# Patch layer of a four-layer network on one Trainium2 core: the product with C is cut in two, the rest is done after the next scan, and two decay buffers become one ring tile

## The chip, the cores and the metric

The kernel runs on one core of a Trainium2 chip. The metric is device time in microseconds (us), from the start to the end of the launch. Five engines work side by side, each in the order of its own queue: PE (matmul), DVE (VectorE: elementwise work and scans), ACT (ScalarE: activations and copies), POOL (GpSimd: elementwise work in SBUF) and SP (here it only issues DMAs). An instruction of one engine that needs another engine's result waits for a semaphore to reach a count.

## The reference, cut to what matters

Four layers are applied to x of shape (8, 96, 64, 64). Only layer 2 (the third), the "patch layer", is touched. It projects x to 192 inner channels, samples them at shifted positions, cuts the image into 256 small patches of 4 by 4 positions and runs a selective scan over the 16 positions of each patch, in four directions k, for 192 channels d and 16 states n:

```
delta = softplus(dts + bias)                        # (patch, k, d, l)
A = -exp(A_logs)                                    # (k, d, n)
def step(hst, inputs):
    ut, dt, bt, ct = inputs
    dA  = exp(dt[..., None] * A)                    # the decay
    hst = hst * dA + (dt * ut)[..., None] * bt      # the scan
    y   = einsum('bkdn,bkn->bkd', hst, ct)          # product with C, summed over the states
    return hst, y
```

Then come a sum over the four directions, a layer norm, a gate and an output projection with a residual.

## The kernel before

All work in fp32. Layer 2 handles 8 images in 8 chunks of 512 positions (32 patches), 64 chunks in all. A chunk has 48 **groups**: 4 directions x 2 halves of the channels x 6 blocks of 16 channels. One group has 128 partitions (16 channels x 8 states) and 1024 columns: two halves of 512, one for states 0 to 7 and one for 8 to 15. Its steps are:

- **dd**: SP starts a 512 KB DMA that spreads delta and delta*u over the 128 partitions (L320), four slots ahead, into one of 5 buffers.
- **decay**: two ACT activations, exp(delta*A), 128x512 each, into a PSUM tile `da` of two banks (L328).
- **dbu**: POOL multiplies delta*u with B (L349), two slots ahead, 6 buffers.
- **scan**: DVE runs one scan over the 1024 columns, in place in `da` (L1453). Directions 2 and 3 run backwards.
- **product**: DVE multiplies the scan's result with C, into `dbu` (L358).
- **total**: PE sums over the states with two matmuls (L366), one slot later.

For three groups of a chunk, called `late`, the scan writes to an SBUF tile `h`, POOL does the product (L354), and the total comes one slot later still.

The order is written out by hand. `Slots.slot(t)` issues slot t: the dd of group t+4, the two decays of group t+1, the side work "join" and "first", the scan of t, the total of t-1, the side work "pe", the total of a late t-2, the side work "act", the dbu of t+2, the late product of t-1, the side work "pool", the product of t, and the side work "dve", "sp", "end". All other steps of the layer (norm, offset convolution, sampling, softplus, gates, output) are side work, put into slots by `sl.at(slot, kind, run)`. Nothing reorders the instructions of an engine; a framework adds the waits between them. It keeps account of who wrote and read each tile.

`da` comes from a pool `psd` with two buffers, so each group's `da` is a tile of its own:

```
g.da = new(self.psd, [128, 2, NW], "ps_d")
```

Layer 0 uses the same class `Slots` for its own scans.

Of the kernel before, what the change touches and what calls it, by code (L numbers as in the profile page):

```python
# [12 lines left out]
AF = mybir.ActivationFunctionType  # L13
ALU = mybir.AluOpType
PSUM = bass.MemoryType.PSUM
# [3 lines left out]
CH = 96  # L19
IH = IW = 64  # L20
NP = IH * IW
NW = 512
NC = NP // NW
DI = 192
HD = 96
NG = 6
# [12 lines left out]
class Names:  # L39


    def __init__(self):
        self.n = 0
# [6 lines left out]
new = Names()  # L50
# [187 lines left out]
LOG_EXP = "natural_log_exp_and_others"  # L238
FAR = 1e25
AHEAD = 4  # L240


def log_exp_tables(S):
# [31 lines left out]
class Slots(Plan):  # L275
# [12 lines left out]

    def __init__(self, S, consts, pool, psd):
        super().__init__(S)
        self.pool, self.psd = pool, psd
        self.red = S.load("k_red", consts)
        self.consts = consts
        self.minus = new(consts, [128, 1], "minus")
        S.nc.vector.memset(self.minus, -1.0)
        self.half = new(consts, [128, 1], "half")
        S.nc.vector.memset(self.half, 0.5)
        self.groups = {}  # L300
# [6 lines left out]
        return a  # L307

    def run(self):
        ts = list(self.plan) + [t + d for t in self.groups for d in (-AHEAD, 1)]  # L310
        with self.S.tc.manual_schedule():
            for t in range(min(ts), max(ts) + 1):
                self.slot(t)

    def slot(self, t):
        nc, G = self.S.nc, self.groups.get
        g = G(t + AHEAD)
        if g:
            g.dd = new(self.pool, [128, 2, NW], "dd", bufs=AHEAD + 1)
            nc.sync.dma_start(  # L320
                g.dd.rearrange("p x l -> p (x l)"),
                g.steps().unsqueeze(1).to_broadcast([GC, HS, 2 * NW]),
            )
        g = G(t + 1)
        if g:
            g.da = new(self.psd, [128, 2, NW], "ps_d")
            for i in range(2):
                nc.scalar.activation(  # L328
                    g.da[:, i, :], g.dd[:, 0, :], AF.Exp, scale=g.a[:, i : i + 1]
                )  # L330
        for what in ("join", "first"):
            self.side(t, what)
        g = G(t)
        if g:
            g.h = new(self.pool, [128, 2, NW], "h", bufs=2) if g.late else g.da
            flat = [v.rearrange("p s l -> p (s l)") for v in (g.h, g.da, g.dbu)]
            g.scan(*flat)
        g = G(t - 1)
        if g and not g.late:
            self.total(g)  # L340
        self.side(t, "pe")
        g = G(t - 2)
        if g and g.late:
            self.total(g)
        self.side(t, "act")
        g = G(t + 2)
        if g:
            g.dbu = new(self.pool, [128, 2, NW], "dbu", bufs=6)
            nc.gpsimd.tensor_tensor(  # L349
                g.dbu, g.dd[:, 1:2, :].to_broadcast([128, 2, NW]), g.b(), ALU.mult  # L350
            )
        g = G(t - 1)
        if g and g.late:
            nc.gpsimd.tensor_tensor(g.dbu, g.h, g.c(), ALU.mult)  # L354
        self.side(t, "pool")
        g = G(t)
        if g and not g.late:
            nc.vector.tensor_tensor(g.dbu, g.h, g.c(), ALU.mult)  # L358
        for engine in ("dve", "sp", "end"):
            self.side(t, engine)  # L360

    def total(self, g):

# [642 lines left out]
def layer2(S, src, dst, st_in, st_out, images):  # L1006
    tc, nc = S.tc, S.nc
    with ExitStack() as ctx:
        cp = ctx.enter_context(tc.tile_pool(name="l2c", bufs=1))
        psd = ctx.enter_context(tc.tile_pool(name="l2q", bufs=2, space=PSUM))  # L1010
        psy = ctx.enter_context(tc.tile_pool(name="l2y", bufs=1, space=PSUM))
        psk = ctx.enter_context(tc.tile_pool(name="l2k", bufs=1, space=PSUM))
        psa = ctx.enter_context(tc.tile_pool(name="l2p", bufs=1, space=PSUM))
# [37 lines left out]
        with tc.tile_pool(name="l2t", bufs=1) as tp:  # L1051
# [10 lines left out]
            for n in range(4):  # L1062
                at = slice(432 * n, 432 * n + 432)
# [35 lines left out]

        fp = ctx.enter_context(tc.tile_pool(name="l2f", bufs=1))  # L1100
        wp = ctx.enter_context(tc.tile_pool(name="l2w", bufs=1))
        sl = Slots(S, cp, wp, psd)
        log_exp_tables(S)
        acol = sl.negative_exp("l2_alog")

# [22 lines left out]
        def turned(v):  # L1128

            return v.rearrange("p (n h w) -> p n w h", h=4, w=4)  # L1130

        def front(ch, b, pad, xs, c, B):
# [22 lines left out]
                nc.gpsimd.memset(pad[:, r, :], 0.0)  # L1155

            sl.at(B - 92, "sp", load)
            sl.at(B - 89, "act", normal)
            if c in (0, NC - 1):
                sl.at(B - 89, "pool", border)  # L1160

            def conv(m, k0, k1):
                def run():
# [24 lines left out]

            for m, slots, last in (
                (0, ((-86, 2), (-85, 2), (-84, 2), (-81, 2), (-80, 1)), -79),  # L1190
                (1, ((-79, 2), (-67, 2), (-66, 1), (-62, 2), (-61, 2)), -60),
            ):
                k = 0
                for t, taps in slots:
                    sl.at(B + t, "pe", conv(m, k, k + taps))
                    k += taps
                sl.at(B + last, "first", conv_out(m))
# [80 lines left out]
            for t, run in (  # L1278
# [2 lines left out]
                (-47, down), (-46, sampled),  # L1281
            ):
                sl.at(B + t, "pool", run)
            sl.at(B - 44, "act", lambda: nc.scalar.copy(xs[:CH, 1, :], turned(xs[:CH, 0, :])))

            def inner(j):


                def pe():
                    ch["pa"] = new(psa, [128, NW], "ps_a")  # L1290
                    nc.tensor.matmul(
                        ch["pa"],
                        wuu.rearrange("c m o -> c (m o)")[:, j * 128 : (j + 1) * 128],
                        xs[:CH, 0, :],
                        start=True,
                        stop=True,
                    )

                def act():
                    if j == 0:  # L1300
                        ch["u"] = new(fp, [128, BLK, NW], "u")
                    nc.scalar.copy(ch["u"][:, j, :], ch["pa"])

                sl.at(B - 23 + j, "pe", pe)
                sl.at(B - 22 + j, "first", act)

            for j in range(BLK):
                inner(j)
# [33 lines left out]
        def pair(ch, xs, n, T):  # L1342
# [37 lines left out]
            def less():  # L1380
                nc.scalar.activation(st["w"], st["w"], AF.Identity, bias=sl.minus)

            for m, run in enumerate((exp, one, ln, less)):
                sl.at(T - 22 + m, "act", run)

            def block(j):
                e, m, w, s = (lambda k=k: st[k][:, j, :] for k in "emws")

                def add():
                    nc.gpsimd.tensor_tensor(m(), m(), s(), ALU.add)  # L1390

                def lost():
                    nc.gpsimd.tensor_tensor(w(), w(), e(), ALU.subtract)

                def delta():
                    if j == 0:
                        pr["d"] = new(fp, [128, BLK, 2, NW], "delta", bufs=2)
                    nc.gpsimd.tensor_tensor(pr["d"][:, j, 0, :], m(), w(), ALU.subtract)

                def delta_u():  # L1400
                    d, du, u = pr["d"][:, j, 0, :], pr["d"][:, j, 1, :], ch["u"][:, j, :]
                    split = lambda v: v.rearrange("p (n w h) -> p n w h", h=4, w=4)
                    if n:
                        nc.gpsimd.tensor_tensor(split(du), split(d), turned(u), ALU.mult)
                    else:
                        nc.gpsimd.tensor_tensor(du, d, u, ALU.mult)

                    v = d.rearrange("p (n l) -> p n l", l=16)
                    edge = DI - j * 128
                    if edge > 0:  # L1410
                        nc.gpsimd.memset(v[: min(edge, 128), :, 0:1], FAR)
                    if edge < 128:
                        nc.gpsimd.memset(v[max(edge, 0) :, :, 15:16], FAR)

                for i, run in enumerate((add, lost, delta, delta_u)):
                    t = BLK * i + j
                    sl.at(T - 18 + t + (t > 4), "pool", run)

            for j in range(BLK):
                first(j)  # L1420
# [3 lines left out]
        def direction(ch, pr, xs, k, n, T):  # L1424
# [52 lines left out]
            for h in range(2):  # L1477
                for g in range(NG):
                    at = 2 * (h * NG + g)
                    sl.groups[T + h * NG + g] = Group(  # L1480
                        n=g, a=acol[:, k, at : at + 2], steps=steps_of(h, g), b=lambda: dr["b"],
                        c=lambda: dr["c"], y=y_of(h, g), scan=scan,
                        late=12 * n + h * NG + g in (2, 26, 34),
                    )

        def end(ch, im, b, c, B):
# [9 lines left out]
            def columns(h):  # L1496
# [9 lines left out]
                        ch["y", h][:HD, :].rearrange("p (n w h) -> p n h w", w=4, h=4),  # L1506
                    )

                sl.at(B + 42 + 6 * h, "pe", pe)
                sl.at(B + 43 + 6 * h, "first", act)  # L1510

            def centred(m):
                def pe():
# [11 lines left out]
                    nc.scalar.copy(ch["yc"][:, m, :], ch["pk"][:HD, :])  # L1525
                    nc.scalar.activation(ch["sq"][:, m, :], ch["pk"][:HD, :], AF.Square)

                sl.at(B + 50 + m, "pe", pe)
                sl.at(B + 51 + m, "first", act)

            def variance():
                ch["pk"] = new(psk, [128, NW], "ps_k")
# [54 lines left out]
                    dst[b][:, c * NW : (c + 1) * NW], ch["xo"].rearrange("c h w -> c (h w)")  # L1587
                )

            sl.at(B + 19, "first", rows(0))  # L1590
            sl.at(B + 25, "first", rows(1))
            for h in range(2):
                columns(h)
                centred(h)
                sl.at(B + 76 + h, "pool", lambda h=h: gated(h))
                sl.at(B + 87 + h, "pe", lambda h=h: out(h))
            for t, engine, run in (
                (53, "pe", variance), (54, "first", root), (55, "dve", scaled),
                (84, "sp", residual), (89, "pe", plus), (90, "first", sum_out),
                (90, "dve", stats), (91, "sp", store),  # L1600
            ):
                sl.at(B + t, engine, run)
            if c == NC - 1:
# [443 lines left out]
```

## Time and profile before

| what | value |
|---|---|
| median of 10 runs (lowest to highest) | 18775.72 us (18755.92 to 18802.76) |
| the profiled execution: time, span | 18779.02 us, 18777.3 us |
| layer 2, from its first scan to its last product | 4175.9 to 14977.6 us, 3072 groups, 3.52 us each |
| DVE, POOL, PE, ACT busy in that stretch of 10801 us | 10456, 10338, 9645, 7366 us |
| one scan, one product, one decay, one dbu | 2288, 1225, 692, 2358 ns |
| DMA share in that stretch | 0.92 |

A group's line in the profile gives the source line, engine, operation, output<-input by tile name, shapes and count, then busy us and mean ns of one, then the engine's idle time before them and what ended it. A line of the timeline gives start, duration, engine, line, operation; neighbouring instructions of a group are merged (x2), and idle time ahead of it stands in brackets with what ended it. Recorded durations reach a little into the next instruction of the same engine.

### The profile page before, as it was taken

What the parts mean: (1) busy time and instruction counts of PE and PEld (TensorE: products, weight loads), DVE (VectorE), ACT (ScalarE), POOL (GpSimd) and SP (SyncE); (2) the same over time, 40 slices, a digit from 0 to 9 for tenths busy, and PEclk for the clock granted to TensorE, in tenths of its full rate; (3) what the DMA queues carried; (4) which work ended last, traced back from release to release, by engine and by line L of the source; (5) the groups of instructions that cost most, each with busy time, mean ns of one, the idle gap of its engine ahead of it and who ended that gap; (6) DMA issues with size and microseconds to landing.
All of it is one profiled execution on the core that took longest, in us unless ns stands there. A gap on an engine that the chain in (4) does not pass through costs nothing. (4 is left out here: it accounts for less than half of the span.)

```text
span 18777.3 us, 133063 instructions
## 1 busy us (share of the span) xinstructions
PE 14644.2 (78%) x34700; PEld 5244.4 (28%) x34700; DVE 16338.5 (87%) x9561; ACT 10722.3 (57%) x17159; POOL 15402.8 (82%) x9600
## 2 busy tenths in 40 slices
PE   8998998858888888898989888888989744343332
PEld 2222223722323233232323223232323211111111
DVE  7999998549999999999999999999999856777667
ACT  7777776436666666666666666666666511111110
POOL 7999996029999999999999999999999855665555
PEclk8999998869999999999999999999999976666666
DMA  7888887349999999999999999999999844444444
GB/s 124 142 144 141 143 142 119 58 108 153 154 154 152 155 152 153 154 153 154 153 153 153 154 152 154 154 153 154 153 153 153 140 141 129 143 142 141 138 138 125
DMA packets 936973, 2689.44 MB, mean 143 GB/s; under 512 B 273907, under 2 KB 275648, under 8 KB 933422
## 3 DMA queue, kind: packets, MB, share of 16 engines
q1 hardware_dynamic: 788749, 2227.79, 70.2%
q0 software_dynamic: 147456, 453.13, 8.0%
q8 instruction: 273, 4.47, 0.1%
q14 instruction: 495, 4.05, 0.1%
HBM read 579.53 MB, written 87.69 MB: 36 GB/s over the span
## 5 line engine op out<-in xcount | busy, mean ns | idle before, releaser
L349 POOL TENSOR_TENSOR dbu<-dd,brep 128x1024 f32<-128x1024 f32 x3840 | 9025.7, 2358 | 481.5 <-DMA dd<-delta 376.8
L366 PE MATMUL ps_y<-dbu,k_red 128*96 128x512 f32 x15360 | 7538.0, 619 | 728.0 <-DVE dbu L358 712.8
L328 ACT ACTIVATE ps_d<-dd,l_alog 128x512 f32<-128x512 f32 x7680 | 5310.9, 692 | 3461.7 <-DVE dbu L358 3289.3
L1453 DVE TENSOR_TENSOR_SCAN ps_d<-ps_d,dbu 128x1024 f32<-128x1024 f32 x2880 | 6590.1, 2288 | 153.4 <-ACT ps_d L328 121.9
L358 DVE TENSOR_TENSOR dbu<-ps_d,crep 128x1024 f32<-128x1024 f32 x3520 | 4312.1, 1225 | 333.4 <-DVE ps_d L1453 7.3
L366 PEld LDWEIGHTS ps_y<-dbu,k_red 128*96 128x96 f32 x15360 | 2360.6, 167 | 5558.8 <-issue 2866.2
L1897 POOL DMA_INDIRECT v<-t,idx x2304 | 2188.7, 950 | 1534.0 <-DVE s L1924 710.2
L1924 DVE TENSOR_REDUCE s<-v 128x864 f32<-128x3456 f32 x256 | 1554.9, 6074 | 435.3 <-remote 401.7
L1915 DVE TENSOR_TENSOR v<-v,ps_w 128x3456 f32<-128x3456 f32 x256 | 958.3, 3743 | 662.8 <-ACT ps_w L1907 631.3
L661 DVE TENSOR_TENSOR_SCAN ps_d<-ps_d,carry,dbu 128x1024 f32<-128x1024 f32 x560 | 1315.0, 2348 | 95.5 <-ACT ps_d L677 78.5
L1943 ACT COPY smp<-ps_t 128x768 f32<-128x768 f32 (+1 forms) x512 | 244.9, 530 | 1686.1 <-remote 1169.6
L1432 PE MATMUL ps_a<-xs,rep_w 96*128 96x512 f32 x2048 | 1110.9, 624 | 36.7 <-ACT brep L1440 30.6
L1168 PE MATMUL ps_k<-pad,woff 96*96 96x512 f32 x2304 | 1094.6, 598 | 34.4 <-ACT pad L1145 20.6
L1935 PE MATMUL ps_t<-k_ident,s 128*128 128x128 f32 (+1 forms) x1792 | 327.6, 334 | 1014.5 <-issue 443.1
L354 POOL TENSOR_TENSOR dbu<-h,crep 128x1024 f32<-128x1024 f32 x320 | 753.5, 2355 | 124.1 <-DVE h L1453 91.3
L1749 PE MATMUL ps_u<-k_ident,oc 27*128 27x27 f32 x256 | 33.4, 254 | 755.6 <-ACT oc L1744 708.9
L1732 PE MATMUL ps_a<-xpad,l_om 96*27 96x512 f32 x1152 | 594.2, 669 | 2.1 <-issue 2.1
L206 POOL TENSOR_TENSOR sc<-bn_ve,mhalf 96x1 f32<-96x1 f32 (+1 forms) x2 | 1.2, 622 | 698.4 <-DVE mv L976 698.3
L1935 PEld LDWEIGHTS ps_t<-k_ident,s 128*128 128x128 f32 (+1 forms) x1792 | 252.4, 170 | 1144.0 <-issue 712.3
L1168 PEld LDWEIGHTS ps_k<-pad,woff 96*96 96x96 f32 x2304 | 372.5, 164 | 674.3 <-issue 587.9
L1432 PEld LDWEIGHTS ps_a<-xs,rep_w 96*128 96x128 f32 x2048 | 345.5, 190 | 755.7 <-ACT brep L1440 319.5
L1966 PE MATMUL ps_o<-smp,l_w 128*96 128x512 f32 (+1 forms) x896 | 461.0, 672 | 73.8 <-ACT smp L1943 71.2
(259 smaller groups left out, 17544.9 us busy)
## 6 DMA issues: line engine op xcount, KB each, us to landing
dd<-delta SPq DMA_DIRECT2D x3840, 512.0 KB
v<-t,idx POOLq DMA_INDIRECT x2304
xo<-x SPq DMA_DIRECT2D x128, 192.0 KB
x<-xo SPq DMA_DIRECT2D x128, 192.0 KB
x<-x SPq DMA_DIRECT2D x16, 1536.0 KB
yr<-y SPq DMA_DIRECT2D x12, 1536.0 KB
xn<-x SPq DMA_DIRECT2D x64, 192.0 KB
xh<-x SPq DMA_DIRECT2D x16, 768.0 KB
```

What stands on the lines that cost most here:

```text
L328: nc.scalar.activation(g.da[:, i, :], g.dd[:, 0, :], AF.Exp, scale=g.a[:, i : i + 1])
L349: nc.gpsimd.tensor_tensor(g.dbu, g.dd[:, 1:2, :].to_broadcast([128, 2, NW]), g.b(), ALU.mult)
L354: nc.gpsimd.tensor_tensor(g.dbu, g.h, g.c(), ALU.mult)
L358: nc.vector.tensor_tensor(g.dbu, g.h, g.c(), ALU.mult)
L366: self.S.nc.tensor.matmul(y, self.red[:, 80 - GC * g.n : 176 - GC * g.n], g.dbu[:, i, :], start=first and i == 0, stop=last and i == 1,)
L661: nc.vector.tensor_tensor_scan(out, da, dbu, carry[:, n : n + 1] if c else 0.0, ALU.mult, ALU.add)
L1168: nc.tensor.matmul(ch["pk"][:HD, :], woff[:, k, m * HD : (m + 1) * HD], pad[:, dy : dy + 8, dx : dx + IW], start=k == 0, stop=k == KT - 1,)
L1432: nc.tensor.matmul(dr["pa"], rep_w[:, k, what, s, :], xs[:CH, k % 2, :], start=True, stop=True,)
L1453: nc.vector.tensor_tensor_scan(out[:, way], da[:, way], dbu[:, way], 0.0, ALU.mult, ALU.add)
L1897: nc.gpsimd.indirect_dma_start(out=st["v"][:, k].rearrange("p q c -> p (q c)"), out_offset=None, in_=flat, in_offset=bass.IndirectOffsetOn ...
L1915: nc.vector.tensor_tensor(v3, v3, ps_w[:, g % 2, j * 4 * KT : (j + 1) * 4 * KT] .unsqueeze(2) .to_broadcast([128, 4 * KT, CH]), ALU.mult,)
L1924: nc.vector.tensor_reduce(st["s"], st["v"].rearrange("p k q c -> p k c q"), mybir.AxisListType.X, ALU.add,)
```

## The change

Per slot of layer 2, and for layer 2 alone (`parts=True`):

1. The product of a group is cut: columns 0 to 911 stay right behind its scan, the last PART = 112 columns are issued in the next slot, after the next group's scan. Groups called `whole` (5 of a chunk) keep one product of 1024 columns. The late groups are other ones (3, 14, 38 in place of 2, 26, 34). So 40 of 48 groups are cut.
2. The two `da` tiles become one tile `ring` of [128, 2, 2, 512] (4 banks); group t+1 uses half `ring[:, t % 2]`.
3. In a slot whose preceding group was cut, the first decay of t+1 stays at the head of the slot, and the second is issued last on ACT, behind the side work "act".
4. The total of every group comes two slots after its scan.
5. Side work is placed anew: the FAR marks at patch edges go from POOL memsets to ACT copies of a constant tile (a slot later); some taps of the second offset convolution, the matmuls and copies of `u`, one step of the second softplus, the copy of `xs`, steps of `end` and the output's statistics move by some slots.

```
-    def __init__(self, S, consts, pool, psd):
+    def __init__(self, S, consts, pool, psd, parts=False):
         super().__init__(S)
-        self.pool, self.psd = pool, psd
+        self.pool, self.psd, self.parts = pool, psd, parts
+        if parts:
+            self.ring = new(psd, [128, 2, 2, NW], "ps_d")
...
-        g = G(t + 1)
+        g, before = G(t + 1), G(t - 1)
+        left = before if self.parts and before and not (before.late or before.whole) else None
         if g:
-            g.da = new(self.psd, [128, 2, NW], "ps_d")
-            for i in range(2):
-                nc.scalar.activation(
-                    g.da[:, i, :], g.dd[:, 0, :], AF.Exp, scale=g.a[:, i : i + 1]
-                )
+            g.da = self.ring[:, t % 2] if self.parts else new(self.psd, [128, 2, NW], "ps_d")
+            self.decay(g, 0)
+            if not left:
+                self.decay(g, 1)
         for what in ("join", "first"):
             self.side(t, what)
...
             g.scan(*flat)
-        g = G(t - 1)
-        if g and not g.late:
+        if left:
+            self.product(left, 2 * NW - PART, 2 * NW)
+        g = G(t - 2 if self.parts else t - 1)
+        if g and (self.parts or not g.late):
             self.total(g)
...
         self.side(t, "act")
+        if G(t + 1) and left:
+            self.decay(G(t + 1), 1)
...
+        self.side(t, "mid")
         if g and not g.late:
-            nc.vector.tensor_tensor(g.dbu, g.h, g.c(), ALU.mult)
+            self.product(g, 0, 2 * NW - PART if self.parts and not g.whole else 2 * NW)
...
+    def decay(self, g, i):
+        self.S.nc.scalar.activation(
+            g.da[:, i, :], g.dd[:, 0, :], AF.Exp, scale=g.a[:, i : i + 1]
+        )
+
+    def product(self, g, lo, hi):
+        o, h, c = (v.rearrange("p s l -> p (s l)")[:, lo:hi] for v in (g.dbu, g.h, g.c()))
+        self.S.nc.vector.tensor_tensor(o, h, c, ALU.mult)
...
-        psd = ctx.enter_context(tc.tile_pool(name="l2q", bufs=2, space=PSUM))
+        psd = ctx.enter_context(tc.tile_pool(name="l2q", bufs=1, space=PSUM))
...
-        sl = Slots(S, cp, wp, psd)
+        sl = Slots(S, cp, wp, psd, parts=True)
+        far = new(cp, [128, NW // 16], "far")
+        nc.vector.memset(far, FAR)
...
-                        late=12 * n + h * NG + g in (2, 26, 34),
+                        late=12 * n + h * NG + g in (3, 14, 38),
+                        whole=12 * n + h * NG + g in (1, 2, 13, 35, 37),
...
-            sl.at(B - 44, "act", lambda: nc.scalar.copy(xs[:CH, 1, :], turned(xs[:CH, 0, :])))
+            sl.at(B - 36, "act", lambda: nc.scalar.copy(xs[:CH, 1, :], turned(xs[:CH, 0, :])))
...
-                    if edge > 0:
-                        nc.gpsimd.memset(v[: min(edge, 128), :, 0:1], FAR)
-                    if edge < 128:
-                        nc.gpsimd.memset(v[max(edge, 0) :, :, 15:16], FAR)
+                def edges():
...
+                    for lo, hi, at in ((0, edge, 0), (edge, 128, 15)):
+                        if lo < hi:
+                            nc.scalar.copy(v[lo:hi, :, at], far[lo:hi])
...
+                sl.at(t + 1, "act", edges)
...
-                (90, "dve", stats), (91, "sp", store),
+                (91, "sp", store),
+                (90, "dve", stats) if c == NC - 1 else (100, "mid", stats),
```

## Prediction

> **What bounds the kernel now.** I read the page's groups first, then the busy times of layer 2's stretch, then the timeline of a few slots. The columns of the second view are the stretch, its length, busy us of PE, PEld, DVE, ACT and POOL (x instructions), the granted clock, DMA share and GB/s.
>
> ```profile
> L349 POOL TENSOR_TENSOR dbu<-dd,brep 128x1024 f32<-128x1024 f32 x3840 | 9025.7, 2358 | 481.5 <-DMA dd<-delta 376.8
> L328 ACT ACTIVATE ps_d<-dd,l_alog 128x512 f32<-128x512 f32 x7680 | 5310.9, 692 | 3461.7 <-DVE dbu L358 3289.3
> L1453 DVE TENSOR_TENSOR_SCAN ps_d<-ps_d,dbu 128x1024 f32<-128x1024 f32 x2880 | 6590.1, 2288 | 153.4 <-ACT ps_d L328 121.9
> L358 DVE TENSOR_TENSOR dbu<-ps_d,crep 128x1024 f32<-128x1024 f32 x3520 | 4312.1, 1225 | 333.4 <-DVE ps_d L1453 7.3
> ```
>
> ```profile
> 4175.00:14976.00 10801.00, 9644.92 (x20754) 3227.58 (x20753) 10456.38 (x6112) 7366.30 (x10509) 10337.72 (x6005) 0.99 0.92 153
> ```
>
> DVE is busy 97% of the stretch and a scan waits for ACT only 122 us of it: DVE sets the pace with scan, product, scan, product. POOL is close behind (96%), ACT has a third of its time free, all of it waiting for DVE's product.
>
> ```profile
> 8998.78 1.23 DVE L358 TENSOR_TENSOR dbu<-ps_d,crep 128x1024 f32<-128x1024 f32 x1
> 8999.92 2.29 DVE L1453 TENSOR_TENSOR_SCAN ps_d<-ps_d,dbu 128x1024 f32<-128x1024 f32 x1
> 9002.32 1.23 DVE L358 TENSOR_TENSOR dbu<-ps_d,crep 128x1024 f32<-128x1024 f32 x1
> 9003.46 2.29 DVE L1453 TENSOR_TENSOR_SCAN ps_d<-ps_d,dbu 128x1024 f32<-128x1024 f32 x1
> ...
> 9005.85 1.23 DVE L358 TENSOR_TENSOR dbu<-ps_d,crep 128x1024 f32<-128x1024 f32 x1
> ...
> 9006.99 2.29 DVE L1453 TENSOR_TENSOR_SCAN ps_d<-ps_d,dbu 128x1024 f32<-128x1024 f32 x1
> 9007.11 1.42 ACT L328 ACTIVATE ps_d<-dd,l_alog 128x512 f32<-128x512 f32 x2 [0.16 <-DVE dbu L358]
> ```
>
> A slot is 3.54 us: the product starts 2.40 after its scan (9002.32 - 8999.92), which it needs, and the next scan 1.14 after the product (9003.46 - 9002.32), before that one's recorded end. In the late group a scan follows a scan after 2.20 (8007.02, 8009.22): the dependent step costs 0.20 more. The decays start 0.03 after the product's end (9005.85 + 1.23 = 9007.08) and run **beside the next scan**, in the other tile `ps_d`. That overlap is what to watch. The start of the layer gives the price of the opposite hand-over, from decay to scan:
>
> ```profile
> 4174.40 1.43 ACT L328 ACTIVATE ps_d<-dd,l_alog 128x512 f32<-128x512 f32 x2
> 4175.93 2.30 DVE L1453 TENSOR_TENSOR_SCAN ps_d<-ps_d,dbu 128x1024 f32<-128x1024 f32 x1 [112.28 <-ACT ps_d L328]
> ```
>
> It is 4175.93 - 4175.83 = 0.10 us.
>
> **The waits that the change brings.** The diff says nothing of waits, since the framework adds them; so I read the semaphore counts in the two built programs. Before, each scan of layer 2 waits for the second decay of its own tile and each product for its own scan. In the changed program the two halves of `ring` are one tile, and each access waits for the last writer of that tile, whichever half it wrote:
>
> ```
> ACT decay 0 of t+1            waits for DVE's product of t-1
> DVE scan of t                 waits for ACT's decay 0 of t+1   (2558 scans; own data were ready earlier)
> DVE last 112 columns of t-1   wait for DVE's scan of t         (2559 of 2560)
> ACT decay 1 of t+1            waits for DVE's 112 columns of t-1
> DVE product of t, 0 to 911    waits for ACT's decay 1 of t+1   (2558 products)
> ```
>
> In the other 513 scans (behind a whole or late group) it is decay 1 of t+1. So the decays no longer run beside the scans: every slot becomes a chain that goes from DVE to ACT and back twice. A present row shows that such waits are kept on the chip: the second decay of a pair waits for the first, though it writes the other half of the tile, and the pair takes 1.42, not less.
>
> **Cost of a slot**, from the end of the product of t-1 to the end of the product of t:
>
> - hand-over to ACT 0.03, decay 0.69, hand-over to DVE 0.10;
> - scan, up to the start of a dependent instruction: 2.40;
> - the 112 columns: the trace has this size nearly (next fence, 272 ns for 108), so 0.28;
> - hand-over 0.03, decay 0.69, hand-over 0.10;
> - product of 912 columns: 1.225 less 112 x 1.04 ns = 1.11 (slope from 108 and 288 columns, 272 and 460 ns).
>
> ```profile
> L1814 DVE TENSOR_TENSOR cl<-f,cl 128x288 f32<-128x288 f32 x14 | 6.4, 460 | 0.2
> ...
> L1814 DVE TENSOR_TENSOR cl<-f,cl 128x108 f32<-128x108 f32 x4 | 1.1, 272 | 0.1
> ```
>
> Sum 5.43 us against 3.54. The 48 slots of a chunk:
>
> - 36 as above: 195.5;
> - 4 whole ones behind a cut group (1, 13, 35, 37), product 1.23: 5.55 each, 22.2;
> - slot 2, whole behind whole (both decays ahead of the scan): 0.03 + 1.42 + 0.10 + 2.40 + 1.23 = 5.18;
> - 3 late (3, 14, 38), no product: 0.03 + 1.42 + 0.10 + 2.29 = 3.84 each, 11.5;
> - 4 cut ones behind a late or whole group (4, 15, 36, 39): 0.03 + 1.42 + 0.10 + 2.40 + 1.11 = 5.06 each, 20.2.
>
> That is 254.6. ACT's side work hides where it fits. Between decay 0 and decay 1 it has 0.10 + 2.40 + 0.28 + 0.03 = 2.81; the fullest hold 1.8 (two roots and a copy of brep, 0.64 + 0.58 + 0.58). In slots 15, 36 and 39, where both decays go first, table loads and an activation (two loads of 1.28, one pass of 1.06, a copy of 0.58 or the eviction of 0.76) make 4.20, 4.38, 4.20 against 0.10 + 2.40 + 1.11 + 0.03 = 3.64: 1.9 over in all. DVE's own side work: the scaling (1206 ns) lies beside decay 0 but for 0.3; the statistics (679 ns) now stand between a scan and its product, 0.4 more than the gap there. A chunk: 254.6 + 1.9 + 0.7 = 257.2 us.
>
> Before, a chunk takes 10801.7 / 64 = 168.8 (first scan 4175.9, last product's end 14977.6). The difference, 88.4, times 64 chunks is 5658 us. The profiled execution took 18779.0 (its span 18777.3), so after: 24437; that execution lies 3.3 above the median of ten, so 24434 on the median.
>
> **What costs nothing, and its cover.** POOL loses 512 memsets of 155 ns and keeps 2358 ns per slot plus side work, 161.5 us of a chunk of 257: it is no longer near the bound. The FAR copies on ACT (512; the nearest row is a 128x144 copy of 285 ns) stand in the 2.81 window of slots that hold under 1.2; uncovered they would cost 512 x 0.285 = 146. PE's totals, a slot later, find `dbu` done; PE needs 9645 / 64 = 151 of 257 us. SP's dd waits for a decay of a group five back, and the DMA engines' share of 0.92 of 3.52 is 3.2 us of a slot of 5.4; SP's loads and stores of chunks keep their slots. The moved taps, copies of u and xs only change which ACT window they fill, counted above. The later totals delay the end of the layer once, by 0 to one slot (5.4). With 5.43 per slot nothing of POOL, PE or DMA is late next: what is late is ACT, twice per slot, by construction.
>
> Bounds of the sum: each of four hand-overs could be 0.03 shorter or longer; the 112 columns lie between the row for 36 columns (196 ns) and that for 288 (460 ns): 0.08 less, 0.18 more. I take 0.28, as 108 columns are nearest. Together -0.20 to +0.30 per slot, over 2560 slots -512 to +768; all terms at one end at once is unlikely.
>
> **Two rules weighed.** The Trainium skill, page "PSUM — Partial Sum Buffer", section "PSUM bank collisions raise a hardware error", says to guard PSUM by bank and quadrant. Each quarter of the ring is a bank of its own, so by that rule nothing would tie the halves together and the sum would be that of the first rival; the semaphore counts are those of whole tiles, so I go by them. The page "VectorE: DVE Perf Modes", section "The DRAIN you can't avoid", says that the next operation does not start until the pipe is empty, with or without a semaphore. The row says otherwise (2.20 against 2.40 behind a scan); by the rule the first rival would gain nothing at all and pay 2560 extra instructions.
>
> **The rivals.**
>
> 1. *The waits do not bind, and the change does what it says* (ends on the other side). The 112 columns follow the scan after 2.20, take 0.18 up to the next start, and the product starts at 2.40 as now but is 0.117 shorter: 2560 x 0.117 = 300 us less, 18479. POOL's 161.5 per chunk would still fit into 164. For it: only that decays in another bank could run beside a scan, as they do now. It decides if decay 0 of t+1 ends before the product of t-1 does, and it cannot, since it waits for that product and the scan waits for it. 3%.
> 2. *Only one of the two ACT steps is exposed.* If decay 0 found its product done 0.8 earlier, 0.03 + 0.69 + 0.10 = 0.82 would go from 2560 slots: 24437 - 2099 = 22338. Against it: both waits stand in nearly every slot. 5%.
> 3. *More than ACT's decays gets into the chain*: copies on ACT that wait for PE stand ahead of decay 1, and PE's granted clock may fall when it idles more (0.99 here, 0.66 in the last layer). 0.5 us in 30 of 48 slots is 960 us: 25400. Against it: PE's results are due a slot earlier. 8%.
>
> **How the numbers follow.** The forecast holds 84%. Of that some 5 lie outside 23850 to 25100, which is the sum with most of its bounds and stops short of rivals 1 to 3 (16%). No change that a measurement can tell is 0.2% (38 us): faster 3%, within 0.2% nothing, slower 97%.
>
> **What would show it.** Right: a scan starting 0.1 after a single decay in nearly each slot; two separate decays of 0.69 instead of a pair; DVE's idle time before scans and products put down to ACT ps_d, 0.8 each, some 2000 us each; scan to scan 5.4; POOL busy under 65% and DMA share near 0.6 in the layer; the 112 columns 2.40, not 2.20, behind the scan. Wrong: decays beside scans, or slots near 3.4. The other layers should keep their times.

## The result, and the profile after

The changed kernel takes 24261.6 us (median of 8 runs, 24224.4 to 24275.8) against 18785.6 for the kernel before (28 runs): ratio 1.2912, 95% interval 1.2900 to 1.2923. The profiled execution took 24252.1 with a span of 24250.4. Layer 2 goes from its first scan at 4151.7 to its last product at about 20444; it took 10801 us and now takes 16293, and these 5491 us are all of the loss (5473 between the two profiled executions). The other layers keep their times within some 25 us.

The page's busy times and its groups that answer to those shown of before:

```profile
PE 16694.1 (69%) x34700; PEld 5795.7 (24%) x34700; DVE 16956.8 (70%) x12122; ACT 10888.4 (45%) x17671; POOL 15371.8 (63%) x9088
...
L361 POOL TENSOR_TENSOR dbu<-dd,brep 128x1024 f32<-128x1024 f32 x3840 | 9009.9, 2350 | 4811.8 <-DMA dd<-delta 3062.8
...
L376 ACT ACTIVATE ps_d<-dd,l_alog 128x512 f32<-128x512 f32 x7680 | 5320.9, 693 | 8811.6 <-DVE dbu L383 8202.6
L1482 DVE TENSOR_TENSOR_SCAN ps_d<-ps_d,dbu 128x1024 f32<-128x1024 f32 x2880 | 6618.7, 2298 | 2781.0 <-ACT ps_d L376 2762.7
L383 DVE TENSOR_TENSOR dbu<-ps_d,crep 128x112 f32<-128x112 f32 (+2 forms) x6080 | 4714.8, 775 | 2249.3 <-ACT ps_d L376 2080.8
...
L1482 DVE TENSOR_TENSOR_SCAN h<-ps_d,dbu 128x1024 f32<-128x1024 f32 x192 | 439.8, 2291 | 302.3 <-ACT ps_d L376 302.3
```

No step of the chain became slower: a scan takes 2298 ns (2288 before), a decay 693 (692), a dbu 2350 (2358). What is new is idle time. DVE stood idle 122 us before scans for ACT's decays (112 of them once, before the layer's first scan); now it stands idle 2763 before scans into `ps_d` (102 of them before the first), 302 before scans into `h` and 2081 before products, together 5146 us, and all of it is put down to one writer, the decay at L376. ACT in turn waits 8203 us for DVE's products. Each engine waits for the other.

The same in layer 2's stretch (columns as in the prediction):

```profile
4175.00:20444.00 16269.00, 11686.20 (x20733) 3782.58 (x20732) 11075.65 (x8663) 7516.92 (x10996) 10284.88 (x5485) 0.85 0.86 101
```

DVE, 97% busy before, is busy 11076 of 16269 us (68%), POOL 63%, PE 72%, ACT 46%. No engine is the bound any more; the chain from one to the other is.

Waits by releaser (idle us, number of waits), first before the scans, then before the products:

```profile
  ACT ps_d L376: 3065.0, 2980
```

```profile
  ACT ps_d L376: 2080.8, 2533
```

Nearly all 3072 scans and nearly all 2560 second parts of a slot wait. A cut slot in the timeline, DVE's and ACT's instructions of the chain:

```profile
9018.60 0.69 ACT L376 ACTIVATE ps_d<-dd,l_alog 128x512 f32<-128x512 f32 x1 [1.18 <-DVE dbu L383]
...
9019.40 2.30 DVE L1482 TENSOR_TENSOR_SCAN ps_d<-ps_d,dbu 128x1024 f32<-128x1024 f32 x1 [0.83 <-ACT ps_d L376]
...
9021.73 0.28 DVE L383 TENSOR_TENSOR dbu<-ps_d,crep 128x112 f32<-128x112 f32 x1
...
9022.10 0.69 ACT L376 ACTIVATE ps_d<-dd,l_alog 128x512 f32<-128x512 f32 x1 [1.31 <-DVE dbu L383]
...
9022.83 1.11 DVE L383 TENSOR_TENSOR dbu<-ps_d,crep 128x912 f32<-128x912 f32 x1 [0.82 <-ACT ps_d L376]
9023.97 0.69 ACT L376 ACTIVATE ps_d<-dd,l_alog 128x512 f32<-128x512 f32 x1 [1.18 <-DVE dbu L383]
...
9024.76 2.30 DVE L1482 TENSOR_TENSOR_SCAN ps_d<-ps_d,dbu 128x1024 f32<-128x1024 f32 x1 [0.83 <-ACT ps_d L376]
```

Nothing of DVE lies beside a decay: decay, scan, 112 columns, decay, 912 columns, decay. Scan to scan is 5.36 us (9024.76 - 9019.40), where it was 3.54.

### The profile page after: what moved, and what is told of

The parts are those of the page before. It is cut to its first block, busy times and chain, and to the rows that moved or that the text cites. A ratio compares the mean times of both kernels' runs of the same rounds, so it can differ in the third digit from the quotient of the medians.

```text
span 24250.4 us, 140596 instructions
## 1 busy us (share of the span) xinstructions
PE 16694.1 (69%) x34700; PEld 5795.7 (24%) x34700; DVE 16956.8 (70%) x12122; ACT 10888.4 (45%) x17671; POOL 15371.8 (63%) x9088
## 5 line engine op out<-in xcount | busy, mean ns | idle before, releaser
L361 POOL TENSOR_TENSOR dbu<-dd,brep 128x1024 f32<-128x1024 f32 x3840 | 9009.9, 2350 | 4811.8 <-DMA dd<-delta 3062.8
L389 PE MATMUL ps_y<-dbu,k_red 128*96 128x512 f32 x15360 | 8926.5, 696 | 1927.0 <-DVE dbu L383 1898.2
L376 ACT ACTIVATE ps_d<-dd,l_alog 128x512 f32<-128x512 f32 x7680 | 5320.9, 693 | 8811.6 <-DVE dbu L383 8202.6
L1482 DVE TENSOR_TENSOR_SCAN ps_d<-ps_d,dbu 128x1024 f32<-128x1024 f32 x2880 | 6618.7, 2298 | 2781.0 <-ACT ps_d L376 2762.7
L383 DVE TENSOR_TENSOR dbu<-ps_d,crep 128x112 f32<-128x112 f32 (+2 forms) x6080 | 4714.8, 775 | 2249.3 <-ACT ps_d L376 2080.8
L389 PEld LDWEIGHTS ps_y<-dbu,k_red 128*96 128x96 f32 x15360 | 2704.9, 189 | 7667.5 <-issue 3908.6
L1461 PE MATMUL ps_a<-xs,rep_w 96*128 96x512 f32 x2048 | 1416.2, 780 | 1099.1 <-ACT brep L1469 703.7
L366 POOL TENSOR_TENSOR dbu<-h,crep 128x1024 f32<-128x1024 f32 x320 | 752.0, 2350 | 1262.7 <-DVE h L1482 1233.1
L1193 PE MATMUL ps_k<-pad,woff 96*96 96x512 f32 x2304 | 1234.7, 658 | 150.8 <-ACT off L1207 140.4
L1377 PE MATMUL ps_a<-xs,wd 97*128 97x512 f32 x768 | 566.1, 827 | 626.6 <-ACT sp_m L1390 440.0
L1461 PEld LDWEIGHTS ps_a<-xs,rep_w 96*128 96x128 f32 x2048 | 395.9, 226 | 2046.3 <-ACT brep L1469 1139.5
L1482 DVE TENSOR_TENSOR_SCAN h<-ps_d,dbu 128x1024 f32<-128x1024 f32 x192 | 439.8, 2291 | 302.3 <-ACT ps_d L376 302.3
L1234 PE MATMUL ps_a<-off,l_off 96*96 96x512 f32 x512 | 355.8, 832 | 304.3 <-ACT u L1327 284.3
```

The lines of the kernel that those rows point to most:

```text
L361: nc.gpsimd.tensor_tensor(g.dbu, g.dd[:, 1:2, :].to_broadcast([128, 2, NW]), g.b(), ALU.mult)
L376: self.S.nc.scalar.activation(g.da[:, i, :], g.dd[:, 0, :], AF.Exp, scale=g.a[:, i : i + 1])
L383: self.S.nc.vector.tensor_tensor(o, h, c, ALU.mult)
L389: self.S.nc.tensor.matmul(y, self.red[:, 80 - GC * g.n : 176 - GC * g.n], g.dbu[:, i, :], start=first and i == 0, stop=last and i == 1,)
L1193: nc.tensor.matmul(ch["pk"][:HD, :], woff[:, k, m * HD : (m + 1) * HD], pad[:, dy : dy + 8, dx : dx + IW], start=k == 0, stop=k == KT - 1,)
L1461: nc.tensor.matmul(dr["pa"], rep_w[:, k, what, s, :], xs[:CH, k % 2, :], start=True, stop=True,)
```

## The experiments

A table of slots serves all of them. It holds the mean time in us from the start of a group's scan to the start of the next one, at places 0 to 47 of a chunk, over the 58 chunks 4 to 61, worked out from the scans' starts in each trace. "Plain" is a slot like most others (cut groups behind cut ones where the kernel cuts): places 20 to 32, without place 26 for `before` and `ring_alone`, which have a late group there.

| kernel | plain | 5 | 7 | 16 | 18 | 37 | 40 | sum of 48 |
|---|---|---|---|---|---|---|---|---|
| before | 3.53 | 3.73 | 4.66 | 3.72 | 3.53 | 3.91 | 3.73 | 168.9 |
| after | 5.37 | 5.37 | 5.30 | 5.36 | 5.37 | 6.21 | 5.38 | 254.6 |
| ring_alone | 5.22 | 5.23 | 5.22 | 5.22 | 5.22 | 5.21 | 5.21 | 247.8 |
| half_decay0 | 5.15 | 5.15 | 5.09 | 5.15 | 5.15 | 5.99 | 5.16 | 244.4 |
| half_decay1 | 5.15 | 5.15 | 5.09 | 5.15 | 5.15 | 5.77 | 5.16 | 244.1 |
| two_tiles | 3.42 | 3.54 | 3.62 | 4.28 | 4.02 | 4.53 | 8.65 | 170.9 |
| two_tiles_uncut | 3.54 | 3.54 | 3.54 | 3.93 | 3.53 | 3.89 | 8.21 | 173.2 |
| late_u | 3.42 | 3.86 | 3.78 | 4.30 | 3.78 | 4.53 | 5.31 | 167.9 |
| fitted | 3.42 | 4.41 | 3.84 | 3.82 | 3.42 | 3.89 | 4.62 | 166.7 |
| fitted_uncut | 3.54 | 3.54 | 3.54 | 3.86 | 3.53 | 3.89 | 4.50 | 169.0 |
| part56 | 3.48 | 3.96 | 3.75 | 3.91 | 3.48 | 3.89 | 4.49 | 167.9 |
| part224 | 3.41 | 4.62 | 3.84 | 3.84 | 3.41 | 3.89 | 4.84 | 166.8 |

`two_tiles`, `two_tiles_uncut`, `ring_alone` and `half_decay1` ran on one chip, where the kernel before took 18778.8. The other six ran on chips where it takes 17960 (17957.5 for `part56` and `part224`). In the traces from there the time behind layer 2's last scan is 2988 to 2999 us, in all others 3802 to 3844; so between the two groups ratios, differences to the kernel before and slots are compared, not times.

**Is it the one tile? `two_tiles`.** The changed kernel with two tiles in place of one ring; all else stays.

```
-            self.ring = new(psd, [128, 2, 2, NW], "ps_d")
+            self.ring = [new(psd, [128, 2, NW], f"ps_d{k}") for k in range(2)]
...
-            g.da = self.ring[:, t % 2] if self.parts else new(self.psd, [128, 2, NW], "ps_d")
+            g.da = self.ring[t % 2] if self.parts else new(self.psd, [128, 2, NW], "ps_d")
```

> The changed kernel with two tiles of two banks in place of the one ring tile; nothing else differs. My theory (the ring is one tile to the framework, so its halves wait for each other): the built program now lets the 112 columns wait for decay 0, done at 0.8 us of the slot, and the product for its own scan. A cut slot is 2.40 + 912 columns (0.95 + 0.07 up to the next start) = 3.42 us against 3.54, so up to 2560 x 0.117 = 300 us under the kernel before: 18485. POOL needs 160.3 of such a chunk of 163 and may give back up to 200: 18485 to 18690. Rival A (the cut itself and the late second decay cost the time, not the ring): stays near 24250. Rival B (a DVE instruction never starts before the one ahead of it is through, so the cut hides nothing): 2560 further instructions of 0.17 us, 435 us slower than before: 19220.

Measured: 18911.2, ratio 1.0058 (1.0040 to 1.0076). Two tiles take away 5350 of the 5483 us between the changed kernel and the one before. Both kernels keep the same data in four banks and issue the same instructions in the same order; only the account of who wrote what is kept in two places. So the one tile is the cause. The rest of the expectation failed: this kernel is still slower than before. First what works, DVE's timeline in a stretch where ACT keeps up (x2 merges the 112 columns and the product behind them):

```profile
9438.33 2.30 DVE L1482 TENSOR_TENSOR_SCAN ps_d<-ps_d,dbu 128x1024 f32<-128x1024 f32 x1 [0.42 <-ACT ps_d L376]
9440.54 1.30 DVE L383 TENSOR_TENSOR dbu<-ps_d,crep 128x112 f32<-128x112 f32 x2
9441.76 2.29 DVE L1482 TENSOR_TENSOR_SCAN ps_d<-ps_d,dbu 128x1024 f32<-128x1024 f32 x1
```

The 112 columns start 2.21 behind the scan, and a plain slot is 3.43 (9441.76 - 9438.33) where it was 3.54. The cut does what it says. What takes the gain back stands a few us earlier in the same trace, and once in every chunk (place 40: 8.65 us):

```profile
9419.70 1.06 ACT L1225 ACTIVATE off<-off 96x1024 f32<-96x1024 f32 x1
...
9422.70 0.58 ACT L1327 COPY u<-ps_a 128x512 f32<-128x512 f32 x1
...
9423.33 3.73 PE L1234 MATMUL ps_a<-off,l_off 96*96 96x512 f32 x4 [4.52 <-ACT u L1327]
...
9429.71 1.88 PE L1234 MATMUL ps_a<-off,l_off 96*96 96x512 f32 x4
...
9431.63 0.58 ACT L1245 COPY fr<-ps_a 96x512 f32<-96x512 f32 x1 [2.64 <-PE ps_a L1234]
...
9432.23 1.28 ACT L1254 ACT_TABLE_LOAD   x1
...
9433.52 1.06 ACT L1254 ACTIVATE fr<-fr 96x1024 f32<-96x1024 f32 x1
...
9434.60 1.28 ACT L1255 ACT_TABLE_LOAD   x1
...
9435.89 0.69 ACT L376 ACTIVATE ps_d<-dd,l_alog 128x512 f32<-128x512 f32 x1
...
9436.62 1.29 DVE L383 TENSOR_TENSOR dbu<-ps_d,crep 128x112 f32<-128x112 f32 x2 [4.61 <-ACT ps_d L376]
```

The third copy of `u`, moved by the change to place 37, reads the PSUM tile `ps_a`. ACT gets to it only behind an activation and two table loads; until then PE cannot write `ps_a`, and its matmuls for the offsets wait 4.52. Not all of that is the copy's: on the mean of the 58 chunks these matmuls start 2.57 behind the end of the activation that writes their input `off`, and 0.05 behind the copy of `u`, so the copy makes some 2.5 of the wait. And it costs more than the wait. While PE stands idle, the clock that it is granted falls to half (0.50, the third figure from the end; columns as in the prediction):

```profile
9423.30:9427.06 3.76, 3.73 (x5) 1.45 (x6) 3.76 (x3) 1.95 (x3) 3.41 (x2) 0.50 0.96 150
```

Four offset matmuls take 3.73 us at half the clock, the next four 1.88. ACT's second copy of their results waits 2.64 for PE, the next activation with its two table loads comes late, the decay behind it as well, and DVE stands 4.61 us. In slots of 5.4 us ACT has the time for all of this: the changed kernel has the same wait (4.51 on the mean) and the same slow matmuls (1.05 each), and its place 40 is not longer than others. In slots of 3.4 it has not.

**The cut or the moved side work? `two_tiles_uncut`.** As `two_tiles`, and no product is cut:

```
-                        whole=12 * n + h * NG + g in (1, 2, 13, 35, 37),
+                        whole=True,
```

> Two tiles, and every product whole: both decays at the head of each slot, no 112 columns behind a scan; the late totals, the FAR copies on ACT and the other moves of side work stay. My theory: these moves cost nothing, so within 0.3% of before, 18730 to 18840, and the difference to the kernel with two tiles and the cut is the worth of the cut. Rival: the moves themselves cost or gain, over 60 us to either side.

Measured: 19050.7, ratio 1.0138 (1.0121 to 1.0155), and above the expectation. This kernel has all the rest of the change (the side work's new places, the later totals, the other late groups) and neither the ring nor the cut, and costs 272 us more than before; its place 40 takes 8.21. So the rest, the moves for short, costs 272 and the cut gives 139 back (19050.7 - 18911.2).

**The ring without the rest: `ring_alone`.** The kernel before, with one tile of four banks:

```
-            g.da = new(self.psd, [128, 2, NW], "ps_d")
+            g.da = self.ring[:, t % 2] if self.ring is not None else new(self.psd, [128, 2, NW], "ps_d")
...
-        psd = ctx.enter_context(tc.tile_pool(name="l2q", bufs=2, space=PSUM))
+        psd = ctx.enter_context(tc.tile_pool(name="l2q", bufs=1, space=PSUM))
...
+        sl.ring = new(psd, [128, 2, 2, NW], "ps_d")
```

> The kernel before, with only the ring tile put in place of the two buffers. My theory: this alone brings most of the loss. Scan waits for the pair of decays, which waits for the product: 0.03 + 1.42 + 0.10 + 2.40 + 1.23 = 5.18 us a slot, 3.84 for the three late ones, some 1.5 of table loads that do not fit: 246 us a chunk against 168.8, so 4940 us more, 23725. Rival (the ring is harmless where no part of a product is left over): 18785.

Measured: 23843.8, ratio 1.2689 (1.2669 to 1.2709). The ring alone makes 5065 us of the loss. DVE's timeline:

```profile
9006.21 2.30 DVE L1454 TENSOR_TENSOR_SCAN ps_d<-ps_d,dbu 128x1024 f32<-128x1024 f32 x1 [1.54 <-ACT ps_d L328]
9008.61 1.23 DVE L358 TENSOR_TENSOR dbu<-ps_d,crep 128x1024 f32<-128x1024 f32 x1
9011.42 2.30 DVE L1454 TENSOR_TENSOR_SCAN ps_d<-ps_d,dbu 128x1024 f32<-128x1024 f32 x1 [1.58 <-ACT ps_d L328]
```

Here both decays stand in one gap of 1.58 before the scan. The cut kernel has two gaps of 0.83 and 0.82 instead, and the 112 columns on top: 5.37 against 5.22 per plain slot. With a ring the cut costs; with two tiles it gains.

**Are both decays on the chain? `half_decay1` and `half_decay0`.** The changed kernel with one of the two decays over 256 columns instead of 512:

```
+        n = NW // 2 if self.parts and i == 1 else NW
...
-            g.da[:, i, :], g.dd[:, 0, :], AF.Exp, scale=g.a[:, i : i + 1]
+            g.da[:, i, :n], g.dd[:, 0, :n], AF.Exp, scale=g.a[:, i : i + 1]
```

(`i == 0` in `half_decay0`. Both also set the ring to zero once, at the start.)

> The changed kernel, but the second decay of every group covers 256 of its 512 columns (the other 256 keep what the buffer held, so the result is not the layer's). Rows of 512 and 1536 columns (692, 1474 ns) give 0.76 ns a column, 0.196 us for 256. My theory (both decays lie on the chain of every slot): 3072 x 0.196 = 600 us less than the changed kernel, 23650. Rival (only the first decay is exposed): no change, 24250.

> The changed kernel with its ring, but the first decay of every group covers 256 of 512 columns (the rest keeps what the buffer held, so the result is not the layer's). The same cut of the second decay took 650 us off the changed kernel's 24250. My theory (the first decay lies on the chain as well, once per slot): 0.196 to 0.215 a slot, 600 to 660 less, 23600. Rival (only one of the two decays is exposed): 24250.

A decay of 256 columns took 478 and 477 ns, one of 512 takes 693: 0.215 less, and 3072 of them are 660 us. Measured: `half_decay1` 23599.4, which is 4821 over its kernel before; `half_decay0` 22779.5, 4819 over its own; the changed kernel stands 5476 over. Each shorter decay saves about 656 us, 99% of its own time, on either side. DVE's timeline of `half_decay0`, then of `half_decay1`:

```profile
9008.69 0.28 DVE L385 TENSOR_TENSOR dbu<-ps_d,crep 128x112 f32<-128x112 f32 x1
9009.78 1.11 DVE L385 TENSOR_TENSOR dbu<-ps_d,crep 128x912 f32<-128x912 f32 x1 [0.82 <-ACT ps_d L378]
9011.50 2.30 DVE L1484 TENSOR_TENSOR_SCAN ps_d<-ps_d,dbu 128x1024 f32<-128x1024 f32 x1 [0.61 <-ACT ps_d L378]
```

```profile
9022.68 0.27 DVE L385 TENSOR_TENSOR dbu<-ps_d,crep 128x112 f32<-128x112 f32 x1
9023.56 1.11 DVE L385 TENSOR_TENSOR dbu<-ps_d,crep 128x912 f32<-128x912 f32 x1 [0.61 <-ACT ps_d L378]
9025.50 2.30 DVE L1484 TENSOR_TENSOR_SCAN ps_d<-ps_d,dbu 128x1024 f32<-128x1024 f32 x1 [0.83 <-POOL bl_d L1274]
```

In the one the gap before the scan shrinks to 0.61, in the other the gap before the product. (The last line names POOL as the releaser; its gap of 0.83 has the size of those put down to the decay.) Both hand-overs are exposed in full.

**Is place 40 the copy of u? `late_u`.** As `two_tiles`, with the third copy of `u` four slots later:

```
-                t = B + (-19, -14, -12)[j]
+                t = B + (-19, -14, -8)[j]
```

> Two tiles with the cut, and the third copy of u moved back out of the way: its matmul from slot 36 to slot 40, its copy from 37 to 41. In the two-tile run slot 40 took 8.65 us where a cut slot takes 3.42, and slots 37 to 39 1.1 more; in it PE's first offset matmul stood 4.5 us behind the copy of u, ACT's chain of offset copies and tanh came late, and the 112 columns of slot 40 waited 4.6 us for decay 0. My theory (the move of u makes that stall): about 4 us of a chunk go, 64 x 4 = 256 less than with two tiles, 18655. Rival (the stall is made by the late group 38, whose short slot leaves ACT no time, or by the totals): no change, 18910.

Measured: 17891.3, ratio 0.9956 (0.9943 to 0.9970), against 1.0058 for `two_tiles`: 201 us less, each against its kernel before, where 256 were expected. Place 40 falls from 8.65 to 5.31. The offset matmuls now start 0.05 behind their input in place of 2.57, and the first four take 0.70 each on the mean in place of 1.08. The copy of `u` was the larger part of the stall there, and one number in the plan moves the kernel from slower than before to faster than before.

**A version that beats both: `fitted`.** As `late_u`; besides, groups 15, 36 and 39 keep one product, and the copies of FAR go one slot later:

```
-                        whole=12 * n + h * NG + g in (1, 2, 13, 35, 37),
+                        whole=12 * n + h * NG + g in (1, 2, 13, 15, 35, 36, 37, 39),
...
-                sl.at(t + 1, "act", edges)
+                sl.at(t + 2, "act", edges)
```

> As before with u moved, and two more fits: groups 15, 36 and 39 whole (so no 112 columns stand in slots 16, 37 and 40, behind ACT's table loads, where they would wait for decay 0), and the FAR copies one slot later (POOL's delta*u is then surely done). My theory (the cut gains 0.117 in each of 37 slots of a chunk once nothing stalls): 3 x 2.20 + 8 x 3.53 + 37 x 3.42 + 1.4 = 163 us a chunk against 168.8, 64 x 5.8 = 370 less than before: 18410; with POOL's 160.3 of 163 some of it may be lost, up to 18600. Rival (POOL and the DMA set the pace once DVE is quicker): 18700 or more.

Measured: 17807.6, ratio 0.9912 (0.9898 to 0.9925): faster than the kernel before by 153 us, where 180 to 370 were expected. The groups with shapes apart:

```profile
L1482 DVE TENSOR_TENSOR_SCAN ps_d<-ps_d,dbu 128x1024 f32<-128x1024 f32 x2880 | 6588.6, 2288 | 281.2 <-ACT ps_d L376 270.3 <-POOL dbu L361 5.8 <-POOL delta L1432 1.7
...
L383 DVE TENSOR_TENSOR dbu<-ps_d,crep 128x112 f32<-128x112 f32 x2368 | 607.3, 256 | 0.0
```

The 112 columns wait for nothing now. What is left is 270 us of scans that wait for decays: 98 once, before the layer's first scan, and 141 at the ends of places 40, 5 and 7 (65, 54 and 23). At 5 and 40 the trace shows copies on ACT in front of the decay that wait for PE. At 40 the wait goes with PE's clock: in the 19 of the 58 chunks in which the granted clock was half for less than 1 us of the 8 us ahead, place 40 takes 3.84, in the other 39 it takes 5.01. Places 5 and 7 were not taken apart like this.

**And without the cut? `fitted_uncut`.** The same with `whole=True`.

> The fitted kernel with every product whole. The difference to the fitted one is the worth of the cut and nothing else. My theory: 45 x 3.53 + 3 x 2.20 + 1.7 = 167.2 us a chunk, 100 us less than before: 18680, and the cut 37 x 64 x 0.117 = 277 us. Rival (the stalls moved, the cut is worth nothing): same as the fitted kernel within 60 us.

Measured: 17968.0, ratio 1.0003 (0.9994 to 1.0012). Not the 100 us less that were expected: the side work's places, mended, are worth nothing by themselves. The whole gain of `fitted` is the cut's, 160 us (277 were expected). From the slots: 31 slots a chunk are 0.115 shorter, 3.6 us; places 5, 7 and 40 take 0.87, 0.30 and 0.12 more. That leaves 2.3 a chunk, 64 times.

**The size of the part: `part56` and `part224`.** `fitted` with another PART:

```
-PART = 112
+PART = 56
```

> The fitted kernel with 56 columns left over in place of 112. Theory (the product needs its scan and cannot start before 2.40 us behind it; columns that need only older data fill the 0.20 us between an independent and a dependent start, and only what was taken off the product is saved): 56 columns take some 0.13 of the 0.20, the product still starts at 2.40 and is 0.058 shorter, so a cut slot is 3.48 and not 3.42; 37 x 64 x 0.058 = 137 us more than fitted, a ratio to before of 0.998 to 1.000. Rival (the gain comes from what else the fitted kernel moves, not from the filled gap): as fitted, 0.991.

> The fitted kernel with 224 columns left over. Theory (the gap of 0.20 us is full at 112 columns): the 224 take 0.30 from 2.21, the product of 800 starts at 2.51 and ends as before, so a cut slot stays at 3.42, while the second decay comes 0.12 later and has no room left where ACT is full: the ratio to before is that of fitted, 0.991, or up to 0.995. Rival (every column moved behind the next scan is saved): another 0.117 a slot, 277 us less, 0.976.

Measured: 17893.2, ratio 0.9963 (0.9950 to 0.9977) with 56 columns, and 17810.9, 0.9915 (0.9902 to 0.9929) with 224. The plain slots are 3.48, 3.42 and 3.41 for 56, 112 and 224 columns, 3.54 for none. `part56` is faster than expected (0.998 to 1.000): its cut slots are as long as forecast, but its place 5 takes 3.96 where that of `fitted` takes 4.41. `part224` came as expected. DVE's timelines, 56 columns and then 224:

```profile
9006.96 2.29 DVE L1482 TENSOR_TENSOR_SCAN ps_d<-ps_d,dbu 128x1024 f32<-128x1024 f32 x1
9009.16 1.36 DVE L383 TENSOR_TENSOR dbu<-ps_d,crep 128x56 f32<-128x56 f32 x2
9010.43 2.29 DVE L1482 TENSOR_TENSOR_SCAN ps_d<-ps_d,dbu 128x1024 f32<-128x1024 f32 x1
```

```profile
9005.81 1.27 DVE L383 TENSOR_TENSOR dbu<-ps_d,crep 128x224 f32<-128x224 f32 x2
9007.00 2.30 DVE L1482 TENSOR_TENSOR_SCAN ps_d<-ps_d,dbu 128x1024 f32<-128x1024 f32 x1
```

The part starts 2.20 behind the scan, the dependent product 2.39 to 2.40. With 56 columns the product still starts there and is shorter by 56 x 1.04 ns = 0.06: 3.54 - 0.06 = 3.48, as measured. With 112 it is shorter by 0.12: 3.42, as measured. With 224 the same sum gives 3.31, and 3.41 is measured: the part no longer fits into the 0.20 and pushes the product back, to 2.50 behind the scan. So 0.20 us can be filled, some 112 columns fill it, and a larger part brings nothing more.

## Why the prediction was right, and where it was off

**The waits: right.** `two_tiles` and `ring_alone` show that the tile's account, and nothing else of the change, makes the chain. Of the two rules weighed, the Trainium skill's guard by bank ("PSUM — Partial Sum Buffer", section "PSUM bank collisions raise a hardware error") says what may not collide; the runs show that the framework's waits were wider than that, by whole tiles, and that the width cost 5350 us. The prediction's sign for it holds too: two decays into one tile, one behind the other, take 1.42, and in `two_tiles` two into different tiles take 1.28 (at 9437.56).

**Two hand-overs per slot, not one: right.** The second rival needed one decay off the chain; the half decays show 99% of each on it.

**The sum: right in total, its terms off.** A plain slot is 5.37, predicted 5.43:

| step | predicted | timeline after |
|---|---|---|
| product to decay 0, decay 0, to the scan | 0.03 + 0.69 + 0.10 | 0.03 + 0.69 + 0.11 |
| scan to the 112 columns | 2.40 | 2.33 |
| 112 columns | 0.28 | 0.28 |
| to decay 1, decay 1, to the product | 0.03 + 0.69 + 0.10 | 0.09 + 0.69 + 0.04 |
| product of 912 | 1.11 | 1.11 |

The 112 columns start 0.07 sooner than the row of the 1024 wide product said, the two hand-overs around decay 1 are as long together as predicted but share it the other way; the last section has the reason for both. 36 such slots are 2.2 us less a chunk. The whole and the late slots came as worked out: place 2 takes 5.24 (5.18), and from scan to scan the late ones take 3.83 to 3.84 (3.84), those before places 2, 14, 36 and 38 6.20 to 6.21 (5.55 and the second decay of the next group, 6.24). Side work in places 15, 36 and 39 costs 4.90 + 5.09 + 4.90 less 3 x 4.37 (5.06 without that second decay), 1.8 against 1.9. The chunk is 254.6 where 257.2 was predicted, 64 x 2.6 = 166 of the 172 us between 24434 and 24262.

**"The moved taps, copies of u and xs only change which ACT window they fill": right here, and only here.** In the changed kernel place 40 is 5.38, like any other. With slots of 3.5 the same moves cost 272 us. The first rival failed on this too: its price of 0.117 per cut slot is right (`part56` and `fitted`), but its 18479 took the moves as free, and with waits that do not bind the change gives 18911, slower than before.

**What would show it: the DMA share was wrong.** The DMA share in the layer is 0.86, not 0.6. Bytes per time fell as the slots grew (153 to 101 GB/s), but the share did not follow. The step that failed is the 3.2 us of DMA time per slot, taken as fixed: the same bytes took longer (last section). The idle time before products (2081 us) and before plain scans (0.83 each) is as predicted; all scans together are nearer 3000 than 2000, since those behind whole and late groups wait for two decays.

**The third rival.** The granted clock of PE did fall in the layer, from 0.99 to 0.85, as the rival had it, and the mean of a total's matmul rose from 619 to 696 ns over the kernel. It did not reach the end: the table above accounts for a plain slot without PE, which is busy 11686 of 16269 us. In the faster kernels the clock does reach it, at place 40.

## What to carry to other kernels

Before two buffers are made halves of one tile, read what the program waits for: if the framework keeps account by tile, a double buffer in one tile is a single buffer, and the engines that used to work side by side take turns. Price side work by the slot length that the change is meant to reach, not by the slow one in front of you: a wait that is hidden at 5.4 us a slot can be the whole loss at 3.4. A gap behind a dependent instruction can be filled only up to its own length (0.20 us here, 112 columns); cut no more than that.

## What the runs showed of the hardware that was not expected

- Behind a scan of 2.29 us an instruction of DVE that does not wait for it starts after 2.20, the 112 columns that wait for it after 2.33, a product of 912 or 1024 columns that waits for it after 2.39 to 2.40. The size is not the reason. An instruction that waits for more than one semaphore has a wait instruction of its own ahead of it in the queue (EVENT_SEMAPHORE in the trace), and that is where the 0.07 lies: in `ring_alone` 2815 products of 1024 columns with one such wait ahead start after 2.40, the 39 products without one after 2.33, as the 112 columns do, which have none.
- The same tells the hand-overs apart. From the 112 columns to a decay it is 0.09 in the changed kernel, where the wait instruction ahead of the decay ends the wait (2494 times), and 0.03 in `two_tiles`, where there is none (2125 times). From a decay to a scan it is 0.10, and the wait instruction runs 0.065 ahead of the scan; from a decay to a product 0.03 to 0.04, and there the wait instruction ran over 1 us earlier.
- The Trainium skill, "VectorE: DVE Perf Modes", section "Two Vector instructions with no wait between them", says that a held instruction starts only when every earlier one has finished. The section that the prediction names, "The DRAIN you can't avoid", says of a next one that is not held that it starts earlier, an exception that the prediction left out. The 2.20, which is 0.09 before the scan's recorded end, agrees with the exception.
- The granted clock of PE falls within a few us of waiting: while PE stood idle from 9418.8 to 9423.3 in `two_tiles` it went from 1.00 to 0.50, and a matmul of 0.59 us took 1.06. So at place 40 PE's wait is paid twice.
- For the same bytes the packets of layer 2 took 1.41 times as long (0.86 x 16269 against 0.92 x 10803 us) when they had more time. The cause is open.
- The kernel before takes 18779 us on one chip and 17960 on others, from which there is no trace of it. In the traces of the other kernels the difference lies in the last layer, from its first gather (DMA_INDIRECT on POOL) to its last (3680 us in `half_decay1`, 2891 in `half_decay0`): on the first chip DVE waits 402 us there for what the profile calls remote (ACT up to 1170 in one place), and in the trace of `fitted`, from another chip, no such wait shows. What the wait is stays open.
